# Context attention in blocks: where queries, keys, values and outputs of the next units stand among the score groups, with the seam and the first weights reordered

## The chip, the cores and the metric

The kernel runs on one core of a Trainium2 chip. A core has five engines that work side by side, each through its own list of instructions in order: TensorE (PE; its weight loads are listed apart as PEld), VectorE (DVE), ScalarE (ACT), GpSimd (POOL) and SyncE (SP, which here issues nearly all DMAs). They wait for one another through semaphores. The metric is the time of one execution in microseconds of the device; smaller is better.

## The reference

One transformer block on x, of 2 batches of 1024 rows of 256 float32 numbers, with 16 heads of 64 in both attentions. The second attention takes its keys and values from a context of 154 rows of 192 per batch.

```python
h = _layernorm(x, ln1_g, ln1_b)
x = _attention(h, h, sa_wq, sa_wk, sa_wv, sa_wo, sa_bo) + x
h = _layernorm(x, ln2_g, ln2_b)
x = _attention(h, cond_emb, ca_wq, ca_wk, ca_wv, ca_wo, ca_bo) + x
h = _layernorm(x, ln3_g, ln3_b)
p = h @ ff_w1 + ff_b1
a, gate = (p[..., :D_FF], p[..., D_FF:])
h = a * jax.nn.gelu(gate, approximate=False) @ ff_w2 + ff_b2
return h + x
```

In `_attention`, softmax(q k^T / 8) weighs v, head by head, and the heads together are multiplied by `wo`.

## The kernel before

All is float32, and the order of every engine's instructions is the order in which the program emits them. The 16 heads go in 8 pairs, so with 2 batches there are 16 *units* (batch, pair) in each attention. The kernel has four parts.

The **prologue** normalizes batch 0 and projects the first queries and keys piece by piece (`part`, `turn`, from L976 on), while weights arrive.

**Self-attention** is a loop over 128 passes p, 8 to a unit (L1026). A pass computes two score tiles (`self_first`), their maxima (DVE) and exponentials (ACT); `exchange` swaps row statistics by four small DMAs on SP; `join` and `scale_groups` put the two halves of a softmax row together (POOL, ACT, DVE); `turn_groups` transposes the probabilities on DVE; `self_values` weighs the values (tile po). Projections for the next unit, output projections and normalization run in between, handed out by `run_work`.

**Context attention** is a loop over 48 slots c, three to a unit (L1050). Each slot has one score group (`cross_first`: tile sc, maxima into neg, exponentials into p; the scaling of p by its reciprocal sums is emitted one slot later, through `lates`). A unit's groups have 3, 3 and 2 row tiles of 128, so 12, 12 and 8 matmul instructions. Two slots later DVE transposes p (`cross_drain`, `cross_turn`) into a ring of three units. Part of the transposed data is moved to other rows by eight DMAs (`cross_regroup`) into a buffer pairs, which is a part of the tile wf and exists once. `cross_values` then weighs the values in two parts of 24 instructions (tile poc). `cross_pieces` builds the next unit's queries (pq, from ca_wq), keys (pk, from ca_wk) and, for every second unit, the values of two units (pv, from ca_wv).

The **feed-forward part** has 64 slots k, each with one gate (pa) and, later, one step of the sum (pf).

What stands beside the score groups comes from four lists: `work` (projections), `side` (steps of a layer norm, some with PE transposes ph), `outs` (output projections py, 8 instructions per row tile) and `later` (DMAs and small additions, two per slot). `run_work(n, n_side, bank, n_sum)` takes up to n PSUM banks' worth of work, then side steps, then outs; `costing` says how many banks a piece takes. Two sets of two PSUM banks are used for this: `mm_tile` and `sum_tile`; score tiles have two more of two banks each. Results leave a bank through `stores` and `adds`, which `flush` emits at fixed places of a slot. In a unit of context attention the order on PE is: first group, pq; second group, poc part 0, pk, py; third group, poc part 1, pv or nothing, py.

An instruction on PE names its operand, its output and the share of the 128 by 128 array it uses: 64*128 for sc and pq (two run side by side in the two halves of the rows), 64*64 for poc and po (four side by side), 96*128 or 128*128 for pk, pv, py, ph and pa, and 96*32 for the second half of pv, whose stationary operand is the last 32 rows of the context. Each float32 product appears as two instructions.

Of the kernel before, what the change touches and what calls it, by code (L numbers as in the profile page):

```python
# [13 lines left out]
P = 128  # L14
# [4 lines left out]
def tile_transformer_block(ctx: ExitStack, tc: tile.TileContext, a: dict, out: bass.AP):  # L19
# [182 lines left out]
    spare = {"bank": mm_tile, "out": mm_tile, "keys": mm_tile}  # L202
# [436 lines left out]
    def self_beside(ui):  # L639

        parts = 2 if 0 < ui < HP else 1
        nxt = self_pieces(*units[ui + 1], parts) if ui + 1 < NU else cross_pieces(*units[0], KB)
# [31 lines left out]
    def self_drain(p):  # L674

        if joins:
            drain.append(scale_groups(*joins.pop(0)))
        if SA < p <= SA + LAG:
            turn_groups(p - LAG - 1)

# [5 lines left out]
    def cross_pieces(b, pr, m=P):  # L686

        t = {}

        def q():  # L690
            t["q"] = p2.tile([P, S], F32, tag="QT", name=f"q_ca{b}_{pr}")
            t["k"] = p2.tile([P, S], F32, tag="KT", name=f"k_ca{b}_{pr}")
            qk["ca", b, pr] = (t["q"], t["k"])
            pq = two_banks(f"pq_ca{b}_{pr}")
            project_both(pq, wsl["ca", pr, "q"], hT["ca", b], m)
            return lambda: take_both(t["q"], pq, scale)

        def keys():
            pk = spare["keys"](f"pk_ca{b}_{pr}")
            for c in range(2):  # L700
                nc.tensor.matmul(
                    pk[:, :T], lhsT=wsl["ca", pr, "k"][:, c, :],
                    rhs=ctxT[:, c, b * TP:b * TP + T], start=(c == 0), stop=(c == 1),
                )
            return lambda: nc.scalar.copy(t["k"][:, :T], pk[:, :T])

        def values():

            v = vs["ca", b, pr // 2] = pt_.tile([P, NM + 2, VC], F32, tag="V", name=f"v_ca{b}_{pr}")
            nc.vector.memset(v[:, NM:, :], 0.0)
            pv = mm_tile(f"pv_ca{b}_{pr}")
            for n, rows_ in ((0, P), (1, KB)):
                for c in range(2):
                    nc.tensor.matmul(
                        pv[:rows_, n * VC:(n + 1) * VC],
                        lhsT=ctxT[:, c, b * TP + n * P:b * TP + n * P + rows_],
                        rhs=wsl["ca", pr, "v"][:, c, :], start=(c == 0), stop=(c == 1),  # L720
                    )

            def store():
                for n in range(NM):
                    own = slice(n * QG, (n + 1) * QG)
                    nc.scalar.copy(v[own, n, :], pv[own, :VC])
                nc.scalar.copy(v[:KB, NM, :], pv[:KB, VC:])
                later.insert(0, lambda: [
                    nc.sync.dma_start(
                        out=v[(1 - n) * QG:(2 - n) * QG, n, :], in_=v[n * QG:(n + 1) * QG, n, :])  # L730
                    for n in range(NM)
                ])
                later.insert(1, lambda: [
                    nc.sync.dma_start(out=v[a4 * KB:(a4 + 1) * KB, NM + a4 % 2, :], in_=v[:KB, NM, :])
                    for a4 in range(1, P // KB)
                ])

            return store

        pieces = [costing(2, q), costing(1, keys)]  # L740
        return pieces + ([costing(1, values)] if pr % 2 == 0 else [])

# [411 lines left out]
```

## Time and profile before

| what | value |
|---|---|
| median of 3 runs | 1149.56 us (1149.43 to 1151.13) |
| profiled execution | 1148.76 us, span 1147.0 us |
| PE busy | 1120.3 us, 98% of the span |
| PE, 200 to 700 us (self-attention) | 500.0 of 500 us |
| PE, 700 to 742 us (seam of the two attentions) | 37.3 of 42 us |
| PE, 780 to 815 us | 33.7 of 35 us |
| PE, 815 to 921 us (inner units of context attention) | 106.0 of 106 us |
| ACT, 815 to 921 us | 59.0 us |
| DVE, 815 to 921 us | 68.1 us |
| DMA share, 780 to 815 us | 0.71 |

The span is the time from the first to the last instruction; the execution's own time has 1.8 us around it. A busy PE need not start its instructions as closely as it can: matmuls overlap, so the distance between starts tells more than the busy time. The timeline gives starts, merged over instructions of one line; the view of waits gives idle time of an engine and what ended it.

### The profile page before, as it was taken

The page shows a single profiled execution, that of the slowest core. Times are in us where ns is not written, and L with a number is a line of the kernel's source. Part 1 is how long each engine was busy: PE and PEld are TensorE (multiplying, and loading weights), DVE is VectorE, ACT ScalarE, POOL GpSimd, SP SyncE. Part 2 cuts the span into 40 slices and gives each one's busy share as a digit, 9 for nine tenths or more (in the row PEclk, how much of TensorE's full clock was granted, in tenths as well). Part 3 has the DMA queues.
Part 4 walks back from the last instruction along what each step waited for, and adds up shares of the span by engine and source line. Part 5 has one row for each costly group of instructions (what it writes and reads, how often), then busy time and mean ns, then how long its engine had stood idle before and what let it go on. Part 6 is the DMA issues. An engine that isn't in the chain of part 4 may idle for free.

```text
span 1147.0 us, 36735 instructions
## 1 busy us (share of the span) xinstructions
PE 1120.3 (98%) x14372; PEld 682.2 (59%) x14372; DVE 833.0 (73%) x1183; ACT 648.6 (57%) x2082; POOL 674.0 (59%) x1568
## 2 busy tenths in 40 slices
PE   8899999999999999999999999999999999999998
PEld 6444444545545545545545554566666667888887
DVE  4888899898898999999899989647666664222222
ACT  4666667666765665676666665637655571041111
POOL 2777777778777777777777777738644453020000
PEclk9999999999999999999999999999999999999999
DMA  2222112101111111111111110267554442000000
GB/s 80 68 71 66 35 32 46 41 13 40 33 29 40 31 31 44 31 31 40 31 31 40 25 28 12 52 141 208 144 120 117 116 88 56 10 10 10 19 10 19
DMA packets 104910, 59.94 MB, mean 52 GB/s; under 512 B 32090, under 2 KB 95522, under 8 KB 104738
## 3 DMA queue, kind: packets, MB, share of 16 engines
q1 hardware_dynamic: 103506, 56.93, 20.8%
q8 instruction: 114, 1.87, 0.7%
q10 hardware_dynamic: 1232, 0.66, 0.2%
q14 instruction: 58, 0.48, 0.1%
HBM read 27.91 MB, written 2.10 MB: 26 GB/s over the span
## 4 chain that ended last, share of the span: by engine, by line
PE 80%; ACT 6%; DMA 3%; DVE 3%; POOL 3%; SPq 2%; issue 2%; DVEq 0%; ACTq 0%; POOLq 0%
PE po L512 15%; PE s L465 15%; PE pa L920 10%; PE py_sa L443 5%; PE py_ca L443 5%; PE pf L943 5%; PE pq_ca L348 5%; ACT p L476 4%; PE pv_sa L379 4%; PE poc L833 4%; PE pk_sa L348 3%; PE pq_sa L348 3%; PE sc L754 3%; DMA st<-st 2%; SPq L486 2%; DVE st L626 2%
## 5 line engine op out<-in xcount | busy, mean ns | idle before, releaser
L476 ACT ACTIVATE p<-s,st 128x512 f32<-128x512 f32 x512 | 345.2, 686 | 203.2 <-DVE st L626 191.5
L577 POOL TENSOR_SCALAR p<-p,rd,ee 128x512 f32<-128x512 f32 x512 | 386.4, 771 | 44.8 <-DVE rd L573 43.9
L626 DVE TENSOR_REDUCE st<-s 128x2 f32<-128x1024 f32 x256 | 301.3, 1218 | 32.9 <-PE s L465 20.1
L591 DVE STREAM_TRANSPOSE pT<-p 128x1024 f32<-128x1024 f32 x256 | 302.1, 1218 | 0.0
L465 PE MATMUL s<-k_sa,q_sa 64*32 64x512 f32 x4096 | 252.1, 594 | 13.5 <-ACT p L476 12.8
L512 PE MATMUL po<-pT,v_sa 64*64 64x256 f32 x4096 | 235.8, 379 | 0.0
L512 PEld LDWEIGHTS po<-pT,v_sa 64*64 64x64 f32 x4096 | 150.4, 133 | 109.1 <-issue 32.8
L781 POOL TENSOR_SCALAR p<-p,rden 128x154 f32<-128x154 f32 x256 | 97.0, 401 | 98.5 <-DVE rden L778 98.0
L465 PEld LDWEIGHTS s<-k_sa,q_sa 64*32 64x32 f32 x4096 | 65.3, 106 | 137.4 <-issue 69.3
L770 ACT ACTIVATE p<-sc,neg 128x154 f32<-128x154 f32 x256 | 96.1, 396 | 79.8 <-DVE rden L778 78.1
L929 DVE SCALAR_TENSOR_TENSOR u<-pa,cols,gate 128x256 f32<-128x256 f32 x64 | 31.0, 484 | 124.4 <-ACT gate L926 124.4
L920 PE MATMUL pa<-hT_ln,wf 128*128 128x256 f32 x512 | 121.0, 379 | 0.0
L926 ACT ACTIVATE gate<-pa,cols 128x256 f32<-128x256 f32 x64 | 30.3, 474 | 151.5 <-PE pa L920 151.5
L920 PEld LDWEIGHTS pa<-hT_ln,wf 128*128 128x128 f32 x512 | 96.8, 190 | 13.7 <-DVE u L929 0.4
L476 ACT ACTIVATION_READ_ACCUMULATOR p<-s,st 128x1 f32 x512 | 103.6, 202 | 0.0
L759 DVE TENSOR_REDUCE neg<-sc 128x6 f32<-128x924 f32 (+1 forms) x48 | 48.4, 1010 | 43.1 <-PE sc L754 43.1
L379 PEld LDWEIGHTS pv_sa<-sa_wv,hT_ln 64*128 64x128 f32 x1024 | 59.3, 188 | 18.7 <-DMA st<-st 9.2
L500 POOL TENSOR_TENSOR zz<-ee,st 128x8 f32<-128x8 f32 x128 | 25.9, 203 | 67.5 <-ACT ee L498 67.5
L943 PE MATMUL pf<-wf,u 128*128 128x256 f32 x256 | 65.0, 379 | 0.2 <-DVE u L929 0.2
L379 PE MATMUL pv_sa<-sa_wv,hT_ln 64*128 64x128 f32 x1024 | 63.3, 276 | 1.7 <-DMA sa_wv<-in_L_xattn_sa_wv_dram 1.4
L443 PE MATMUL py_ca<-ca_wo,o_ca 128*128 128x256 f32 x256 | 60.8, 384 | 0.3 <-ACT hT_ln L281 0.3
L348 PE MATMUL pq_ca<-hT_ln,ca_wq 64*128 64x512 f32 (+1 forms) x304 | 60.5, 591 | 0.2 <-ACT hT_ln L281 0.2
(87 smaller groups left out, 1243.6 us busy)
## 6 DMA issues: line engine op xcount, KB each, us to landing
wf<-pT_ca SPq DMA_DIRECT2D x128, 128.0 KB, 2.4
st<-st SPq DMA_DIRECT2D x512, 1.0 KB, 1.8
v_sa<-v_sa SPq DMA_DIRECT2D x32, 256.0 KB, 3.5
sa_wq<-in_L_xattn_sa_wq_dram SPq DMA_DIRECT2D x32, 128.0 KB, 2.9
sa_wk<-in_L_xattn_sa_wk_dram SPq DMA_DIRECT2D x32, 128.0 KB, 2.8
sa_wv<-in_L_xattn_sa_wv_dram SPq DMA_DIRECT2D x32, 128.0 KB, 3.0
ca_wq<-in_L_xattn_ca_wq_dram SPq DMA_DIRECT2D x32, 128.0 KB, 3.1
wf<-in_L_xattn_ff_w_dram SPq DMA_DIRECT2D x12, 256.0 KB, 3.7
```

The costliest lines, as they stand in the source:

```text
L348: nc.tensor.matmul(pq[r][f:f + m, at:at + n], lhsT=wt[own, c, f:f + m], rhs=h[own, c, t0:t0 + n], start=(c == 0), stop=(c == NH - 1), tile ...
L379: nc.tensor.matmul(pv[r][:, i * P:(i + 1) * P], lhsT=h[own, c, i * P:(i + 1) * P], rhs=wt[own, c, :], start=(c == 0), stop=(c == NH - 1), ...
L443: nc.tensor.matmul(py[:, :D], lhsT=o[:, i, t * P:(t + 1) * P], rhs=wo[kind][:, half * HP + i, :], start=(i == 0), stop=(i == HP - 1),)
L465: nc.tensor.matmul(sc[a4 * KB:(a4 + 1) * KB, j, :], lhsT=q[r, c:c + KB], rhs=k[r, h * HB:(h + 1) * HB], start=True, stop=True, tile_positi ...
L476: nc.scalar.activation(pr[:, j, :], sc[:, j, :], AF.Exp, bias=st[:, 0, 0, i, j:j + 1], accum_out=st[:, 0, 1, i, j:j + 1],)
L512: nc.tensor.matmul(po[a2][j * DH:(j + 1) * DH, :QH // 2], lhsT=v[r, t, e, j * DH:(j + 1) * DH], rhs=pT[r, j * NK + n, :], start=(t == 0 an ...
L577: nc.gpsimd.tensor_scalar(pr[:, j, :], pr[:, j, :], rd[:, c:c + 1], ee[:, 0, c:c + 1], op0=ALU.mult, op1=ALU.mult,)
L591: nc.vector.transpose(halves[h][:, :, c:c + KB], groups.pop(0).rearrange("p j (n k) -> p (j n) k", k=KB))
L626: nc.vector.tensor_reduce(st[:, 0, 0, i, :], sc[i], AX.X, ALU.max, negate=True)
L781: nc.gpsimd.tensor_scalar(pr_[:, j, i, :T], pr_[:, j, i, :T], rden[:, j, i:i + 1], 1.0, op0=ALU.mult, op1=ALU.mult,)
L920: nc.tensor.matmul(pa[:, half, :TF * P], lhsT=w1[:, c, half * DF + f * P:half * DF + (f + 1) * P], rhs=h[:, c, t0 * P:(t0 + TF) * P], star ...
L943: nc.tensor.matmul(sums[blk][i][:, :D], lhsT=sums[blk, "u"][:, f, i * P:(i + 1) * P], rhs=w2[:, f, :], start=(f == 0), stop=(f == NF - 1),)
```

## The change

In context attention the pieces of the next unit leave `work` and stand at fixed places. The queries are computed behind the first score group of a unit. The keys come right behind the second group, and after them a norm step, the values (`context_values`, in every second unit, now for this unit and the next), two output projections, and both parts of `cross_values`; the second part takes its banks from the other set. The third group has only a norm step behind it, and output projections where more than two are waiting. The second half of pv takes the last 128 context rows instead of the last 32, and its last 32 output rows (rows 96 to 127) are kept. All eight DMAs of `cross_regroup` are issued in the third slot of the next unit. The loads of key and value weights move to the third slot. Two layer norms are queued earlier, by one unit each.

At the seam, unit 1's keys come before the first score group; the queries of units 1 and 2 behind the second and third group; the last two parts of self-attention's values behind the fourth and fifth; and the last transposes of self-attention on other places. At the start, unit 1's value weights of self-attention are loaded at the end of pass 2 and not in pass 3, one x tile goes one pass later, and in the prologue `part("k", 1)` stands before `turn[3]`.

```diff
-            halves[h, "po"] = [sum_tile(f"po_{h}_{a2}") for a2 in range(2)]
+            bank = sum_tile if h < 2 * NU - 1 else mm_tile
+            halves[h, "po"] = [bank(f"po_{h}_{a2}") for a2 in range(2)]
...
+    def cross_queries(b, pr, m=P, bank=mm_tile):
+        q = qk["ca", b, pr, "q"] = p2.tile([P, S], F32, tag="QT", name=f"q_ca{b}_{pr}")
+        pq = [bank(f"pq_ca{b}_{pr}_{r}") for r in range(2)]
+        project_both(pq, wsl["ca", pr, "q"], hT["ca", b], m)
+        return lambda: take_both(q, pq, scale)
+
+    def cross_keys(b, pr, bank=mm_tile):
+        k = qk["ca", b, pr, "k"] = p2.tile([P, S], F32, tag="KT", name=f"k_ca{b}_{pr}")
+        pk = bank(f"pk_ca{b}_{pr}")
+        for c in range(2):
+            nc.tensor.matmul(
+                pk[:, :T], lhsT=wsl["ca", pr, "k"][:, c, :],
+                rhs=ctxT[:, c, b * TP:b * TP + T], start=(c == 0), stop=(c == 1),
+            )
+        return lambda: nc.scalar.copy(k[:, :T], pk[:, :T])
+
+    def context_values(b, pr):
...
+        for n, k0 in enumerate((0, TP - P)):
+            for c in range(2):
+                nc.tensor.matmul(
+                    pv[:, n * VC:(n + 1) * VC], lhsT=ctxT[:, c, b * TP + k0:b * TP + k0 + P],
...
+        last = P // KB - 1
...
+            nc.scalar.copy(v[last * KB:, NM + last % 2, :], pv[last * KB:, VC:])
...
     def cross_regroup(c):
 
+        ui, n = divmod(c - len(CG) - 2, len(CG))
+        if n != 0 or not 0 <= ui < NU:
+            return
         for a2 in range(2):
-            ui, n = divmod(c - len(CG) - 2 - a2, len(CG))
-            if n != 0 or not 0 <= ui < NU:
-                continue
...
-        po = {a4: sum_tile(f"poc_{ui}_{a4}") for a4 in quarters}
+        po = {a4: (mm_tile if a2 else sum_tile)(f"poc_{ui}_{a4}") for a4 in quarters}
...
     def cross_beside(ui):
 
-        if ui + 1 < NU:
-            for what in "kv" if ui else "":
-                load_weights("ca", units[ui + 1][1], what)
-            pieces = cross_pieces(*units[ui + 1])
-            work.extend(pieces[:2])
-            held.extend(pieces[2:])
-        if ui == 3:
+        if ui == 2:
             norm_beside("ca", B - 1)
         if ui > HP + 1:
             ob, oh = divmod((ui - HP - 2) // HP, 2)
             t0 = ((ui - HP - 2) % HP) * 2
             out_pieces("ca", ob, oh, (t0, t0 + 1))
-        if ui == NPAIR + HP + 1:
+        if ui == NU - 4:
             norm_beside("ff", 0)
...
     def cross_weigh(c):
 
-        for part in range(2):
-            ui, n = divmod(c - len(CG) - 4 - part, len(CG))
-            if n == 0 and 0 <= ui < NU:
+        ui, n = divmod(c - 2 * len(CG) - 1, len(CG))
+        if n == 0 and 0 <= ui < NU:
+            for part in range(2):
                 run(lambda: cross_values(ui, part))
+            flush(stores)
...
         part("q", 1)
         emit(normalize[3])
         copies()
+        part("k", 1)
         copies = turn[3]()
-        part("k", 1)
...
-        later.append(tiles[0])
-        later.append(lambda: load_weights("sa", units[1][1], "v"))
-        later.extend(tiles[1:] + chunks)
+        later.extend([lambda: None] + tiles + chunks)
...
                 run_work(2 if p < SA - SH else 1, h % 2 or h == 0, sum_tile)
+                if p == LAG:
+                    load_weights("sa", units[1][1], "v")
...
-            if c % len(CG) == 0:
-                cross_beside(c // len(CG))
-            elif c % len(CG) == 1 and 1 <= c // len(CG) < NU - 2:
-                load_weights("ca", units[c // len(CG) + 2][1], "q")
-            if c % len(CG) == len(CG) - 1:
-                work.extend(held)
-                held.clear()
+            ui, n = divmod(c, len(CG))
+            nxt = units[ui + 1] if ui + 1 < NU else None
+            if n == 0:
+                cross_beside(ui)
+            elif n == 1 and 1 <= ui < NU - 2:
+                load_weights("ca", units[ui + 2][1], "q")
+            elif n == 2:
+                for i, what in ((2, "k"), (1, "v")):
+                    if 1 < ui + i < NU:
+                        load_weights("ca", units[ui + i][1], what)
+            if c == 0:
+                run(lambda: cross_keys(*nxt))
             flush(adds)
             then = cross_first(c)
             flush(stores)
+            if c == 1:
+                turn_groups(SA - 2)
+            if n == 1 and ui > 1 and nxt:
+                run(lambda: cross_keys(*nxt, sum_tile))
+                flush(stores)
             flush(drain)
             flush(lates)
             lates.append(then())
-            if c <= SH:
-                self_drain(SA + c)
+            if c == 0:
+                drain.append(scale_groups(*joins.pop(0)))
+            if c == 2:
+                turn_groups(SA - 1)
+            cross_drain(c)
+            if c == 1:
+                run(lambda: cross_queries(*nxt))
+            elif c == 2:
+                run(lambda: cross_queries(*units[2], bank=sum_tile))
+            elif c == 3:
+                run(lambda: self_values(2 * NU - 1, 0))
+            elif c == 4:
+                run(lambda: self_values(2 * NU - 1, 1))
+                run(lambda: cross_keys(*nxt, sum_tile))
+            elif n == 0 and ui:
+                if nxt:
+                    run(lambda: cross_queries(*nxt))
+                run_work(0, 1)
+            elif n == 1:
+
+                run_work(0, 1, sum_tile)
+                if ui % 2 == 0:
+                    run(lambda: context_values(*units[ui]))
+                run_work(0, 0, n_sum=1)
+                run_work(1, 0)
+                flush(adds)
+                flush(stores)
+                cross_weigh(c)
+            elif n == 2:
+                run_work(0, 1, sum_tile)
+                if len(outs) > 2:
+                    run_work(2, 0)
             cross_regroup(c)
-            cross_drain(c)
-            cross_weigh(c)
-            flush(stores)
-            if c == 1:
-
-                spare["keys"] = sum_tile
-                run_work(3, 0)
-                spare["keys"] = mm_tile
-            elif c > 1:
-                run_work(2, 1, n_sum=2 * (SH < c < 2 * NPAIR and c % len(CG) == 0))
-            if SH - LAG < c <= SH:
-                run(lambda: self_values(2 * NU - 1, c - SH + LAG - 1))
...
-            if k == 3 * len(CG):
+            if k == 3 * len(CG) - 1:
                 norm_beside("ff", B - 1)
-            cross_regroup(c)
             cross_drain(c)
             cross_weigh(c)
-            flush(stores)
+            cross_regroup(c)
             if k == 0:
                 out_pieces("ca", B - 1, 0, range(NT - 2 * TF, NT))
-            if k == len(CG) + 2:
+            if k == len(CG) + 1:
                 out_pieces("ca", B - 1, 1, range(NT))
-            if k > len(CG) + 2:
+            if k > len(CG) + 1:
                 for _ in range(min(2, len(gated) - 1)):
                     run(sum_slot)
                 flush(stores)
```

More of the change, by code (lines that the diff above doesn't have):

```diff
@@ L200, in tile_transformer_block @@
     hT, vs, qk, oT = {}, {}, {}, {}
-    spare = {"bank": mm_tile, "out": mm_tile, "keys": mm_tile}
+    spare = {"bank": mm_tile, "out": mm_tile}
     added = set()
@@ L641, in self_beside @@
         parts = 2 if 0 < ui < HP else 1
-        nxt = self_pieces(*units[ui + 1], parts) if ui + 1 < NU else cross_pieces(*units[0], KB)
+        nxt = self_pieces(*units[ui + 1], parts) if ui + 1 < NU else cross_pieces(*units[0])
         if ui + 1 < NU:
@@ L672, in load_ahead @@
             load_weights("ca", units[1][1] if p == SA - 2 else units[2][1], "kq"[p - SA + 2])
[L674 to L679, printed above, removed]
     CG = [(t, min(TG, NT - t)) for t in range(0, NT, TG)]
@@ L684, in tile_transformer_block @@
     crossed, pTc = {}, {}
[L686 to L699, printed above, removed]
+    def cross_queries(b, pr, m=P, bank=mm_tile):
[3 more added lines that the diff above has]
+        return lambda: take_both(q, pq, scale)
@@ new lines, in cross_keys @@
+    def cross_keys(b, pr, bank=mm_tile):
[8 more added lines that the diff above has]
+    def context_values(b, pr):
+        v = vs["ca", b, pr // 2] = pt_.tile([P, NM + 2, VC], F32, tag="V", name=f"v_ca{b}_{pr}")
+        nc.vector.memset(v[:, NM:, :], 0.0)
+        pv = mm_tile(f"pv_ca{b}_{pr}")
+        for n, k0 in enumerate((0, TP - P)):
@@ L700, in keys @@
             for c in range(2):
                 nc.tensor.matmul(
-                    pk[:, :T], lhsT=wsl["ca", pr, "k"][:, c, :],
-                    rhs=ctxT[:, c, b * TP:b * TP + T], start=(c == 0), stop=(c == 1),
-                )
[L705 to L738, printed above, removed]
@@ L740, in cross_pieces, with store @@
-        pieces = [costing(2, q), costing(1, keys)]
-        return pieces + ([costing(1, values)] if pr % 2 == 0 else [])
+                    pv[:, n * VC:(n + 1) * VC], lhsT=ctxT[:, c, b * TP + k0:b * TP + k0 + P],
+                    rhs=wsl["ca", pr, "v"][:, c, :], start=(c == 0), stop=(c == 1),
+                )
+        last = P // KB - 1
+        def store():
+            for n in range(NM):
+                own = slice(n * QG, (n + 1) * QG)
+                nc.scalar.copy(v[own, n, :], pv[own, :VC])
+            nc.scalar.copy(v[last * KB:, NM + last % 2, :], pv[last * KB:, VC:])
+            later.insert(0, lambda: [
+                nc.sync.dma_start(
+                    out=v[(1 - n) * QG:(2 - n) * QG, n, :], in_=v[n * QG:(n + 1) * QG, n, :])
+                for n in range(NM)
+            ])
+            later.insert(1, lambda: [
+                nc.sync.dma_start(
+                    out=v[a4 * KB:(a4 + 1) * KB, NM + a4 % 2, :],
+                    in_=v[last * KB:, NM + last % 2, :])
+                for a4 in range(last)
+            ])
@@ L743, in cross_first, with cross_pieces @@
+        return store
+    def cross_pieces(b, pr):
+        return [costing(2, lambda: cross_queries(b, pr, KB)), costing(1, lambda: cross_keys(b, pr)),
+                costing(1, lambda: context_values(b, pr))]
     def cross_first(c):
@@ L747, in cross_first @@
         t0, nt = CG[n]
-        q, k = qk["ca", b, pr]
-        k = k[:, :T]
+        q, k = qk["ca", b, pr, "q"], qk["ca", b, pr, "k"][:, :T]
         sc = ps_s.tile([P, 2, HB], F32, tag="s", name=f"sc_{c}")
```

## The prediction

> **What bounds the kernel now.** I read the page first: one core, TensorE clock at full speed in every slice, so time is instructions and waits.
>
> ```profile
> span 1147.0 us, 36735 instructions
> PE 1120.3 (98%) x14372; PEld 682.2 (59%) x14372; DVE 833.0 (73%) x1183; ACT 648.6 (57%) x2082; POOL 674.0 (59%) x1568
> ```
>
> PE is the bound; a change pays only if it takes waits out of PE or makes its instructions start closer together. The view of waits comes next, for PE alone:
>
> ```profile
> PE s L465 <- ACT p L476: 12.8, 22, 1.6
> PE sc L754 <- ACT k_ca L705: 2.3, 1, 2.3
> PE ph_ln L266 <- POOL xn_ln L253: 2.2, 3, 1.1
> PE pv_sa L379 <- DMA sa_wv<-in_L_xattn_sa_wv_dram: 1.4, 2, 1.0
> ```
>
> Two belong to what is changed: 2.3 us at the seam, for context keys, and 1.4 us at the start, for value weights. The rest must come from closer starts, so I read PE's timeline over one inner context unit (score groups at 849.55, 853.87, 858.65). Columns: start, busy time, line, output<-inputs, rows*columns of the array, operand.
>
> ```profile
> 849.55 1.06 PE L754 MATMUL sc<-k_ca,q_ca 64*128 64x154 f32 x12
> 850.43 3.60 PE L348 MATMUL pq_ca<-hT_ln,ca_wq 64*128 64x512 f32 x16
> 853.87 0.95 PE L754 MATMUL sc<-k_ca,q_ca 64*128 64x154 f32 x12
> 854.75 1.09 PE L833 MATMUL poc<-wf,v_ca 64*64 64x256 f32 x16
> 855.66 0.61 PE L833 MATMUL poc<-pT_ca,v_ca 64*64 64x256 f32 x8
> 856.21 0.79 PE L701 MATMUL pk_ca<-ctxT,ca_wk 96*128 96x154 f32 x4
> 856.83 1.89 PE L443 MATMUL py_ca<-ca_wo,o_ca 128*128 128x256 f32 x8
> 858.65 0.79 PE L754 MATMUL sc<-k_ca,q_ca 64*128 64x154 f32 x8
> 859.38 1.09 PE L833 MATMUL poc<-wf,v_ca 64*64 64x256 f32 x16
> 860.29 0.61 PE L833 MATMUL poc<-pT_ca,v_ca 64*64 64x256 f32 x8
> 860.84 2.11 PE L717 MATMUL pv_ca<-ca_wv,ctxT 96*128 96x256 f32 x8
> 862.88 1.99 PE L443 MATMUL py_ca<-ca_wo,o_ca 128*128 128x256 f32 x8
> 864.80 1.06 PE L754 MATMUL sc<-k_ca,q_ca 64*128 64x154 f32 x12
> ```
>
> Read differences of starts. Eight py take 1.82 us behind pk (856.83 to 858.65) but 1.92 behind pv (862.88 to 864.80). In the FF stage, among full-array neighbours only, sixteen take 3.45 (985.68 to 989.13), so eight 1.73. The excess is paid where the array's division changes.
>
> **Term 1, changes of division.** Call F full (96 or 128 rows, 128 columns: pk, pv, py, ph, pa), R 64*128 (sc, pq), Q 64*64 (poc, po). Leaving F costs 1.82 - 1.73 = 0.09; entering F 1.92 - 1.82 = 0.10. Twelve sc take 0.88 behind py and before pq; 24 take 1.67 (719.50 to 721.17), so twelve alone are 0.79, entering R costs 0.10 (rounded up), and leaving it as much (0.88 at 853.87). Sixty-four po take 3.61 (732.93 to 736.54) and 24 poc 1.46, so 0.215 per four; 24 without edges would be 1.30, edges 0.16: by the single starts 0.05 in, 0.11 out. Hence F to R or R to F 0.20, R to Q or F to Q 0.15, Q to F or Q to R 0.21. The second half of pv is 96*32: pv and py from 860.84 to 864.80 take 3.96, against 1.73 twice plus 0.19 of edges, 3.65: 0.31 for the narrow half, gone in the new code, where both halves have 128 columns.
>
> An inner unit now changes six times: F-R, R-Q, Q-F, F-R, R-Q, Q-F = 1.12, plus 0.31 where it has pv. The new order is sc, pq, sc, pk, (pv), py, py, poc twice, sc: R-F, F-Q, Q-R = 0.56, and none at the border of units, where sc meets sc. Where a py pair or a transpose stands behind the third group, two more, 0.40. Following the lists of work through all units from 742 to 948: now 31 F-R, 28 R-Q, 28 Q-F, 4 R-F, one Q-R and seven narrow halves, 19.4 us; new 6 F-R, 21 R-F, 14 F-Q, 14 Q-R, 10.4. That is -9.0. In the FF stage two visits of poc instead of four save 2 x 0.36 = -0.7.
>
> The Trainium skill, "TensorEngine Tiling (Array Packing)", Key Properties, says that changing the tiling mode drains the TensorE; "TensorE: Matmul & The Clock Gate", Part 2, puts a drain at about 128 cycles of 2.4 GHz. By an estimate from those pages the 54 changes saved are 54 x 53 ns = 2.9 us; the rows make it 9.6, and the sum keeps the rows. Against the change, Part 3 of the second page has weight loads overlap with running matmuls only in other row groups, and Part 2 makes them proportional to columns: by that estimate the wider pv half would add (128 - 32)/1.2 ns x 4 x 7 = 2.2 us. The trace disagrees: full py and pa start 0.216 us apart, each with its 0.19 us load hidden.
>
> **Term 2, waits from 742 to 948.** PE's stretch is 206.1 us. Its work without edges, counts by the starts above (228 sc pairs x 0.131, 13 pq x 3.43, 13 pk x 0.53, 7 pv and 28 py x 1.73, 28 poc x 1.30, 8 ph x 0.43), is 181.5; with 19.4 of edges, 5.2 of waits are left, nearly all beside the two layer norms (780 to 815, 921 to 948). New ones: sc of group three and of the next unit's first group are adjacent, so ScalarE has the exponentials of both in a row. VectorE puts a maximum (0.80), a reciprocal and a transpose pair (1.2) before the second maximum (1.12): those exponentials start 3.6 us into the unit instead of 2.3 (864.80 to 867.14), take 2.2, and the query copies (0.56 each) follow. pv wants the bank of the first copy, free at 6.4; PE arrives at 0.79 + 3.43 + 0.88 + 0.63 = 5.7. So 0.65 in four inner units with pv, 2.6 in all; without pv the sum bank of py covers it. The norm steps come in as many slots, and one starts a unit earlier: I take 3.4 for theirs. In all 6.0, +0.8; bounds 2 and 12.
>
> What hides the rest: the moved poc copies (0.72 a part, VectorE) end before pq needs those banks, 0.8 us later; were they late, PE would wait one copy, 0.36, a unit. The memset, the value copies and their five DMAs (the last chunk now from rows 96 to 127, same sizes) have a unit and a half before poc reads them. On SP, all eight regroup issues now stand in one row behind the end of poc, past the loads of k and v; four took 2.62 at 856.93, so eight 5.2, and landing 2.4 (page) makes 7.6. The next poc comes 10.0 (no pv) later: cover 2.4 us. Behind the regroup on SP waits the query load, wanted 10 us on. POOL keeps its order and all instructions.
>
> **Term 3, the seam: 0.** Keys of unit 1 now come before the first score group, so PE waits for their weights:
>
> ```profile
> 718.72 1.48 SPq L120 DMA_DIRECT2D ca_wk<-in_L_xattn_ca_wk_dram  x1
> ...
> 728.51 1.06 PE L754 MATMUL sc<-k_ca,q_ca 64*128 64x154 f32 x12 [2.29 <-ACT k_ca L705]
> ```
>
> PE is there at 719.50. The 512-byte packets of that load run from 721.0 to 721.8, so pk starts near 722.1: a wait of 2.6 in place of 2.29, with everything behind it queued on PE. Bounds: 720.7 (2.0 after issue, the 64 KB copies of v_ca) and 724.71, where pk ran without waiting. Then pk, two sc, pq, sc, pq, sc end at 732.6; po needs the last self-attention transposes. Their chain (exponential 727.4, reciprocal 728.5, four POOL scalings 3.02, transposes) ends at 732.9: 0.3 more. po, sc, po, pk bring the third group of unit 1 to 741.85, now 741.86. The swapped banks (queries of unit 2 in sum banks, the last po in the others) are free 2 us ahead. Bounds -1.5 and +2.
>
> **Term 4, the start: -1.6.** The load of unit 1's value weights moves from behind the fourth exchange on SP (issued 44.10) to behind the third (37.74). PE then does not wait 0.40 + 0.97; but the fourth exchange is issued 0.5 later, and score pass 6 needs the exponentials behind it: -1.0 (0 to -1.4). The one x tile loaded later is wanted four passes on. In the prologue part k 1 moves ahead of the fourth transposes, into waits of 0.1 and 0.19 and past one pair of edges: s starts at 17.85 instead of 18.44, -0.6 (0 to -0.7). From 200 to 700 PE has no gap, so a lead stays.
>
> **Sum.** -9.0 - 0.7 + 0.8 + 0 - 1.6 = -10.5. The profiled execution took 1148.76 (span 1147.0 and 1.8 around it), giving 1138.3; the shown median, 1149.56, lies 0.8 above: 1139.1.
>
> **Rivals.** (a) Slower: the eight regroup issues come late for poc. With the slowest four (3.63 at 742.02) twice and the longest landing in the trace, 5.7 (ca_wk), it is 13.0 against 10.0 or 11.7: waits of 3.0 and 1.3 by turns, 14 units, 30 us: 1169. It decides from 0.75 us a unit, a landing 11.6 us after poc. For: one queue, DMA up to 74% busy. Against: that load falls on units 2 to 5, where most have 4 us more. Chance 0.09. (b) ScalarE becomes the bound of the unit: 0.8 us of waiting in all 13 units with pq, +10.4 less the 2.6 counted: 1147, or no change with term 4 lost, 1149. Against: ScalarE is busy 59.0 of 106 us there. Chance 0.10. (c) Half the good: norm waits double (+3.4), keys' weights land late (+2), start unmoved (+1.6): 1146. Chance 0.18. (d) The change of division costs nothing when queues refill: then only terms 3 and 4, 1148; the repeated start differences speak against. 0.03. Forecast: 0.60.
>
> **How the numbers follow.** 0.2% (2.3 us) is what can be told from no change. The forecast's own bounds: waits of 2 and term 4 at -2.1, seam -1.5, give 1133; waits of 12, no gain at the start and seam +2 give 1148.7. That holds (b) and (c) too; I take 1133.5 to 1148.5 and leave out (a) and the ends. Faster: forecast, (c), most of (b): 0.85; same: (d) and the rest of (b), 0.05; slower: (a) and the tail, 0.10.
>
> **What would show it.** Right: poc x48 in one run, no 96*32 loads, sc followed by sc; an inner unit pair of about 27.7 us instead of 28.5; PE idle before pk near 720; no pv_sa wait on DMA. Wrong: PE waits on DMA before poc, on the ACT query copy before pv beyond 1 us, or pv longer than 1.83.

## The result, and the profile after

The changed kernel is slower. Its median is 1153.77 us (1152.21 to 1154.88), beside 1149.49 us (1147.95 to 1151.13) for the kernel before: a ratio of 1.0039, 95% interval 1.0026 to 1.0052. A second comparison, at the end of the experiments, gave 1.0041 (1.0026 to 1.0055). The loss of 0.4% is small, but clear of the noise. Predicted were 1139.1 us, a ratio of 0.991, and a range from 1133.5 to 1148.5 us. All ratios here are of fast executions; one slow execution of 3067 us, of the kernel with the norm step behind the values, is left out of its ratio.

The page of the changed kernel: the span is 4.9 us longer, and PE is busy 3.9 us *less*. So PE waits more; it does not work more.

```profile
span 1151.9 us, 36754 instructions
PE 1116.4 (97%) x14372; PEld 687.6 (60%) x14372; DVE 836.3 (73%) x1183; ACT 646.6 (56%) x2082; POOL 675.9 (59%) x1568
```

The view of PE's waits after the change (engine, line, releaser: total us, times, longest):

```profile
PE poc L825 <- ACT hT_ln L281: 5.8, 3, 3.0
PE pv_ca L706 <- ACT q_ca L363: 2.9, 6, 1.2
PE pk_ca L690 <- DMA ca_wk<-in_L_xattn_ca_wk_dram: 2.3, 1, 2.3
PE pv_sa L379 <- ACT k_sa L371: 1.3, 1, 1.3
```

The first of these is new and large: the weighing of the values waits three times for a *layer norm's* copies. It lies in units 4, 5 and 15. Here are units 4 and 5 (timeline: start, busy, engine, line, and in brackets the wait ahead and what ended it):

```profile
784.61 0.60 PE L266 MATMUL ph_ln<-ident,xn_ln 128*128 128x128 f32 x4
...
788.23 1.60 ACT L281 ACTIVATE hT_ln<-ph_ln,cols 128x128 f32<-128x128 f32 x4
789.88 1.22 PE L825 MATMUL poc<-wf,v_ca 64*64 64x256 f32 x10 [1.73 <-ACT hT_ln L281]
...
801.45 0.60 PE L266 MATMUL ph_ln<-ident,xn_ln 128*128 128x128 f32 x4
...
804.40 1.66 ACT L281 ACTIVATE hT_ln<-ph_ln,cols 128x128 f32<-128x128 f32 x4
806.11 0.86 PE L825 MATMUL poc<-wf,v_ca 64*64 64x256 f32 x10 [2.99 <-ACT hT_ln L281]
```

The transposes ph end at 785.2, but ScalarE takes them out of their bank only from 788.23 on: the copies stand on its list behind the query copies, the key copy and six exponentials. That bank is one of the two summing banks, and the first part of poc needs both.

In the kernel before, the transposes of such a step take a bank of the other set and stand *behind* the first part of poc, and neither part waits:

```profile
786.52 1.09 PE L833 MATMUL poc<-wf,v_ca 64*64 64x256 f32 x16
...
788.60 0.60 PE L266 MATMUL ph_ln<-ident,xn_ln 128*128 128x128 f32 x4
...
789.86 1.09 PE L833 MATMUL poc<-wf,v_ca 64*64 64x256 f32 x16
```

A second loss follows. Stretches of time in the same place (columns: busy time of PE, PEld, DVE, ACT, POOL, then the granted clock, DMA share, GB/s):

```profile
780.00:790.00 10.00, 7.90 (x52) 4.82 (x52) 6.71 (x16) 9.51 (x41) 9.60 (x26) 1.00 0.89 236
790.00:800.00 10.00, 10.00 (x86) 5.98 (x88) 6.04 (x13) 4.70 (x22) 5.20 (x13) 0.83 0.58 136
800.00:810.00 10.00, 6.60 (x70) 4.12 (x66) 3.26 (x7) 6.05 (x27) 4.17 (x13) 0.87 0.84 195
```

The clock was granted in full everywhere in the profile before. After the change the trace's clock record drops to one half for 3.413 us from 790.3 and again from 807.3, right behind the two waits, and once in the start, from 97.4.

The inner unit, on the other hand, is what the prediction said (same view as its unit of before):

```profile
838.12 1.58 PE L746 MATMUL sc<-k_ca,q_ca 64*128 64x154 f32 x20
839.53 3.60 PE L348 MATMUL pq_ca<-hT_ln,ca_wq 64*128 64x512 f32 x16
842.97 0.95 PE L746 MATMUL sc<-k_ca,q_ca 64*128 64x154 f32 x12
843.85 0.79 PE L690 MATMUL pk_ca<-ctxT,ca_wk 96*128 96x154 f32 x4
844.97 1.99 PE L706 MATMUL pv_ca<-ca_wv,ctxT 96*128 96x256 f32 x8 [0.33 <-ACT q_ca L363]
846.80 3.62 PE L443 MATMUL py_ca<-ca_wo,o_ca 128*128 128x256 f32 x16
850.35 1.09 PE L825 MATMUL poc<-wf,v_ca 64*64 64x256 f32 x16
```

Such double score groups (the third group of a unit and the first of the next, 20 instructions) start at 825.47, 838.12 and 853.10: a pair of units takes 27.63 us, against 28.47 before and 27.7 predicted.

Every run below is placed by one table of *offsets*: the start of the same PE instruction in the run's profiled execution, minus its start in that of the kernel before (us from each span's start). Negative is earlier. "Pass 127" is the last pass of self-attention, c a slot of context attention (12 and 18 enclose units 4 and 5; 42 begins unit 14), "ff 0" the first gate. The last column is where the clock record drops to one half within the program, each time for 3.41 us (6.83 where marked *); a drop at the very end of the program is left out.

| kernel | pass 127 | c=5 | c=12 | c=18 | c=42 | ff 0 | end | half clock from |
|---|---|---|---|---|---|---|---|---|
| changed | +1.15 | +0.86 | -2.03 | +4.56 | +0.74 | +4.38 | +4.93 | 97, 790, 807 |
| changed, again | +1.43 | +2.32 | -0.56 | +6.87 | +3.00 | +6.61 | +7.17 | 35, 185, 724, 792, 806* |
| norm step behind | +0.76 | +0.26 | -0.13 | -2.11 | -1.70 | -0.51 | +0.04 | 97, 704 |
| norm copies first | -1.24 | -0.08 | -2.97 | -2.32 | -5.97 | -4.05 | -3.50 | 722 |
| waits filled | +0.83 | +0.38 | -2.51 | +0.69 | -3.17 | +0.44 | +1.00 | none |
| ff outputs moved | +0.10 | -0.56 | -3.44 | +3.91 | +0.04 | +3.65 | +3.04 | 35, 789, 803* |
| single column | -0.46 | -1.49 | -3.80 | +4.58 | +3.03 | +7.15 | +8.30 | 35, 789*, 806 |
| before, new start | +0.14 | +0.23 | +0.23 | +0.22 | +0.22 | +0.20 | +0.20 | 35 |
| before, new prologue | +2.40 | +3.99 | +3.99 | +3.98 | +3.98 | +3.96 | +3.96 | 35, 185, 731 |
| before, wide pv | +1.38 | +1.30 | +0.87 | +0.60 | -0.35 | -0.05 | -0.05 | none |
| three moves | +1.87 | +2.92 | +0.04 | +0.69 | -5.53 | -2.95 | -3.57 | 725 |
| and keys earlier | +2.90 | +0.69 | -2.19 | -1.54 | -7.13 | -2.87 | -3.48 | 97, 186, 923 |
| last version | +2.99 | +0.51 | -2.37 | -1.43 | -7.63 | -5.69 | -6.30 | 35, 185 |

For the changed kernel: +1.15 in the start, -0.29 in the seam, -2.89 to unit 4, +6.59 in units 4 and 5, -3.82 in units 6 to 13, +3.64 in units 14 and 15, +0.55 behind. The two large losses are where a layer norm runs.

### The profile page after: what moved, and what is told of

Same layout as the page of the kernel before. It is cut to its first block, busy times and chain, and to the rows that moved or that the text cites. A ratio compares the mean times of both kernels' runs of the same rounds, so it can differ in the third digit from the quotient of the medians.

```text
span 1151.9 us, 36754 instructions
## 1 busy us (share of the span) xinstructions
PE 1116.4 (97%) x14372; PEld 687.6 (60%) x14372; DVE 836.3 (73%) x1183; ACT 646.6 (56%) x2082; POOL 675.9 (59%) x1568
## 3 DMA queue, kind: packets, MB, share of 16 engines
q8 instruction: 114, 1.87, 0.7%
## 4 chain that ended last, share of the span: by engine, by line
PE 80%; ACT 7%; DVE 4%; DMA 3%; issue 2%; POOL 2%; SPq 2%; DVEq 0%; ACTq 0%; POOLq 0%
PE po L512 17%; PE s L465 17%; PE pa L907 10%; PE py_sa L443 5%; PE pf L930 5%; PE py_ca L443 4%; PE pk_sa L348 4%; PE pq_sa L348 4%; PE poc L825 4%; PE pv_sa L379 4%; ACT p L476 3%; PE pq_ca L348 3%; ACT p L762 2%; PE sc L746 2%; DMA st<-st 2%
## 5 line engine op out<-in xcount | busy, mean ns | idle before, releaser
L773 POOL TENSOR_SCALAR p<-p,rden 128x154 f32<-128x154 f32 x256 | 97.4, 404 | 101.2 <-DVE rden L770 100.7
L762 ACT ACTIVATION_READ_ACCUMULATOR p<-sc,neg 128x1 f32 x256 | 59.8, 233 | 0.0
L443 PE MATMUL py_ca<-ca_wo,o_ca 128*128 128x256 f32 x256 | 58.3, 381 | 1.3 <-DVE o_ca L838 1.0
```

Source lines behind the costliest of these rows:

```text
L443: nc.tensor.matmul(py[:, :D], lhsT=o[:, i, t * P:(t + 1) * P], rhs=wo[kind][:, half * HP + i, :], start=(i == 0), stop=(i == HP - 1),)
L762: nc.scalar.activation(pr_[:, j, i, :T], sc[:, j, i * T:(i + 1) * T], AF.Exp, bias=neg[:, j, i:i + 1], accum_out=den[:, j, i:i + 1],)
```

## The experiments

The **theory**, formed from the profile above: a summing bank is held by norm transposes whose copies queue behind exponentials ("held bank"), and the waits cost clock besides. The **rival**: ScalarE has too much work there, so any reordering only moves the wait (the prediction's rival (b), at the norm units).

### The norm step behind the values

```diff
-                run_work(0, 1, sum_tile)
                 if ui % 2 == 0:
                     run(lambda: context_values(*units[ui]))
...
                 cross_weigh(c)
+                run_work(0, 1, sum_tile)
```

> The changed kernel, but the norm step of a unit's second slot (transposes into a summing bank) stands behind the two joined visits of values instead of ahead of them. Theory 'held bank': in units 4, 5 and 14 the first visit waits for a bank that the transposes hold until ScalarE has copied them out, and ScalarE does that behind six exponentials. The waits 1.73, 0.42, 2.99 and 1.07 us ahead of the visits go (6.2 us), and with them the two half-speed stretches of 3.41 us at 788 and 805 us that follow them (1.7 us each): 1153.8 - 6.2 - 3.4 = 1144.2 us, between 1142 and 1147. Rival 'ScalarE too slow': from 742 to 948 us the work on ScalarE is too much for the time, so the wait only moves to the next reader of ScalarE; 1152 to 1154 us.

Measured: 1150.88 us, ratio 1.0002 (0.9992 to 1.0012). About 4 us of the 9.6 came. The waits of poc for the norm are gone, and with them the half clock at 790 and 807: units 4 and 5 went from +6.59 to -1.98. But a unit earlier (c=5 to c=12) 2.5 us were lost again, and between c=18 and c=42 another 4.2, of which 2.4 are waits ahead of c=42. None of these waits had been there; the longest of each place:

```profile
780.09 0.66 PE L266 MATMUL ph_ln<-ident,xn_ln 128*128 128x128 f32 x4 [1.85 <-POOL xn_ln L253]
...
919.07 0.33 PE L266 MATMUL ph_ln<-ident,xn_ln 128*128 128x128 f32 x1 [1.35 <-ACT xn_ln L256]
```

A step transposes what the step before it normalized. Moved back, it stands only one score group behind that step, and the normalization (on POOL for this layer norm, on ScalarE for the next) isn't done. The place was wrong, not the theory: ScalarE has the same work here and lost nothing by it in units 4 and 5.

### The norm step in its place, its copies ahead of the exponentials

```diff
             if n == 1 and ui > 1 and nxt:
                 run(lambda: cross_keys(*nxt, sum_tile))
                 flush(stores)
+            if n == 1 and c > SH:
+                run_work(0, 1, sum_tile)
+                flush(stores)
             flush(drain)
             flush(lates)
             lates.append(then())
```

> The changed kernel with the norm step of the second slot still ahead of the values and in the same summing bank, but issued before the group's exponentials, so that ScalarE copies the transposes out first and then takes the exponentials. It parts two causes inside 'held bank'. If it is the queue on ScalarE (copies behind six exponentials, about 3.5 us) that keeps the bank, the waits ahead of the visits go as in the run with the step moved behind: 1144 to 1147 us, less good by up to 2 us because the exponentials start 1.6 us later. If the bank is too short whatever the order, the first visit still waits over 1 us in units 4 and 5 and the time is 1151 to 1154 us. 'ScalarE too slow' gives 1152 to 1154 us here too.

Measured: 1145.18 us, ratio 0.9952 (0.9938 to 0.9966), the ScalarE work being the same. This parts the causes: it is the *order* on ScalarE. (PE's list is the same. The step's few instructions on VectorE and POOL come earlier too; that it is the copies which freed poc is read from the rows.) The copies now come from 785.07 on, 0.8 us behind the transposes, and what is left of the waits in units 4 and 5 is this, but for 0.41 us on the key copy:

```profile
784.63 1.99 PE L706 MATMUL pv_ca<-ca_wv,ctxT 96*128 96x256 f32 x8 [0.36 <-ACT q_ca L363]
785.07 1.57 ACT L281 ACTIVATE hT_ln<-ph_ln,cols 128x128 f32<-128x128 f32 x4
...
789.88 0.87 PE L825 MATMUL poc<-wf,v_ca 64*64 64x256 f32 x10 [1.38 <-ACT v_ca L716]
...
800.87 0.86 PE L825 MATMUL poc<-wf,v_ca 64*64 64x256 f32 x10 [0.75 <-ACT hT_ln L281]
```

The next in line in unit 4 is the second part of poc, which waits for the values' copies, now behind the exponentials themselves. Units 4 and 5 give +0.65 in place of +6.59, units 14 and 15 +1.92 in place of +3.64; 2.4 us of this profile's lead are from the start (pass 127), of which more below.

### The waits filled with idle work

```diff
+                if ui in (4, 5):
+                    fill = mm_tile(f"fill_{c}")
+                    for _ in range(12 if ui == 4 else 22):
+                        nc.tensor.transpose(fill[:, :P], ident, ident)
                 cross_weigh(c)
```

> The changed kernel with 12 and 22 transposes of a constant, whose result nobody reads, put ahead of the joined visits of units 4 and 5, in a bank of the other kind, so that TensorE works through the two waits of 1.73 and 2.99 us. Nothing is made earlier. Theory 'idle costs clock': the two stretches at half clock (3.41 us each, at 788 and 805 us) come from these waits; filled, the clock stays whole there and the time falls by 2 x 1.7 = 3.4 us to 1150.4, with up to 1 us taken back where the filling lasts longer than the wait (1150 to 1152). Rival 'the clock falls for another reason': the half-speed stretches stay, and the time is 1153.8 to 1155.

Measured: 1150.40 us, ratio 0.9995 (0.9987 to 1.0004). Windows as above, and the waits that are left:

```profile
790.00:800.00 10.00, 10.00 (x103) 6.72 (x95) 7.23 (x16) 6.44 (x29) 6.46 (x17) 1.00 0.53 119
800.00:810.00 10.00, 8.95 (x99) 6.31 (x99) 4.87 (x11) 5.42 (x26) 3.87 (x12) 1.00 0.94 216
...
789.38 0.86 PE L825 MATMUL poc<-wf,v_ca 64*64 64x256 f32 x10 [0.41 <-ACT hT_ln L281]
...
803.89 0.86 PE L825 MATMUL poc<-wf,v_ca 64*64 64x256 f32 x10 [1.05 <-ACT hT_ln L281]
```

The granted clock is 1.00 in both, and units 4 and 5 cost +3.20 instead of +6.59: 3.4 us less, as expected, though not one useful instruction was made earlier. These two waits cost twice: their length, and 1.7 us of slow clock each.

### A price for a change of the array's division

```diff
+        if a2:
+            k = P if ui % 2 == 0 else QG
+            nc.tensor.matmul(
+                po[a2][:k, NT * KB:NT * KB + 1], lhsT=ident[:k, :k], rhs=ident[:k, :1],
+                start=True, stop=True, **({} if k == P else {"tile_position": (0, 0)}),
+            )
```

> The changed kernel with one matmul of a single column between the two joined visits of every unit: over the whole array (128 by 128) in even units, over a quarter of it (64 by 64, as the visits themselves) in odd units. It is a price for a change of the array's division by itself. Theory 'edges cost': the quarter-sized one costs its own issue, some 0.05 us; the whole one costs that and two changes, 0.35 to 0.45 us, so the two visits together last about 0.35 us longer in even units than in odd ones, and the program about 8 x 0.4 + 8 x 0.05 = 3.6 us longer (waits aside). Rival 'edges cost nothing': even and odd units alike within 0.1 us.

Measured once, 1157.05 us, which tells nothing finer than the profile does. The same single column between the two parts, over the whole array and over a quarter:

```profile
850.93 1.09 PE L831 MATMUL poc<-wf,v_ca 64*64 64x256 f32 x16
...
852.39 0.38 PE L822 MATMUL poc<-ident 128*128 128x1 f32 x2
...
854.16 1.58 PE L746 MATMUL sc<-k_ca,q_ca 64*128 64x154 f32 x20
...
864.06 1.09 PE L831 MATMUL poc<-wf,v_ca 64*64 64x256 f32 x16
...
865.41 0.16 PE L822 MATMUL poc<-ident 64*64 64x1 f32 x1
...
866.91 1.58 PE L746 MATMUL sc<-k_ca,q_ca 64*128 64x154 f32 x20
```

From poc to sc it is 3.23 us in the even unit and 2.85 in the odd one; the plain visit takes 2.75 (850.35 to 853.10 above). So a quarter-sized matmul costs 0.10 and a whole one 0.48. The difference, 0.38, is at most the price of the two changes, where the prediction's prices give 0.21 + 0.15 = 0.36. Part of it may be the whole matmul's own: its two instructions start 0.13 us apart, each with its weight load, and those of the quarter 0.03. Without that it is 0.28. Rival (d), no price at all, is out either way.

### The context values alone

```diff
-            for n, rows_ in ((0, P), (1, KB)):
+            for n, k0 in enumerate((0, TP - P)):
```

(the kernel before, with the copies and DMAs of the last rows as in the change)

> The kernel before with the context values' last 32 rows computed by a matmul over the whole array (128 rows that overlap the first 128) instead of one over 32 columns of it; nothing else. By rows of the profile before, the narrow matmul had a change of division behind it, so the 8 visits save about 0.3 us each, of which the prediction took 2.2 us in all: 1147.3. By the rule that four times the weights' columns take four times as long to load, it would lose 2.2 us: 1151.7. If the visits' time is hidden or the same either way: 1149.3 to 1149.7.

Measured: 1148.31 us, ratio 0.9986 (0.9977 to 0.9995), 1.6 us faster. In its trace pv and py of an inner unit take 1.83 + 1.82 = 3.65 us, where they took 3.96 before and 3.65 was predicted; the offset falls by 0.31 a visit in the inner units. By the estimate that spoke against the wider pv it would have been slower.

### The start

Two kernels: the kernel before with the whole new start (the x tile one pass later too; the weights at the end of pass 2, the third), and with its prologue alone.

```diff
+        part("k", 1)
         copies = turn[3]()
-        part("k", 1)
...
+                if p == LAG:
+                    load_weights("sa", units[1][1], "v")
```

> The kernel before with the changed start alone (the second key part ahead of the fourth turn in the prologue; the first value weights loaded at the fifth pass instead of with the first loads). In the changed kernel's profile the start is 0.9 us early in the prologue and 1.15 us late from pass 35 on, with a half-speed stretch at 95 to 98.6 us. Theory 'the start costs': 1149.5 + 1.15 = 1150.6 us, between 1150.2 and 1151.5, with that half-speed stretch there again. Rival 'the prediction's': the weights' wait of 1.0 us and 0.6 us of the prologue are gained, 1147.9. Rival 'chance of that execution': no difference, 1149.3 to 1149.7.

> The kernel before with the second key part ahead of the fourth turn alone, the loads as before. Parts the two halves of the start. If the late pass 9 to 15 comes from the moved weights, this keeps the gain of the prologue, 0.6 to 0.9 us: 1148.6 to 1148.9. If the earlier prologue itself shifts the exchange of bytes between partitions into the loads and so costs the half-speed stretch, it is 1150 to 1151.5 as the whole start is.

Measured: 1150.13 us, ratio 1.0009 (0.9997 to 1.0020), and 1150.47 us, ratio 1.0001 (0.9993 to 1.0010). Neither is told from no change; the gain that the prediction took, to 1147.9, is excluded for the whole start, a cost of 1.1 us is not. The first score does start earlier in every profile with the new prologue (by 0.4 to 0.9 us), but the lead does not last. Eleven profiles with the whole new start, the same instructions up to pass 123, stand from -1.24 to +2.99 us at pass 127. One with the old start, that of the wide pv, stands at +1.38. So the +1.15 of the changed kernel, and the 2.4 us by which the run with the copies first led there, are within what one execution and the next differ by, and not to be put down to the change. The half-speed column shows much of the chance: the stretches at 35, 97 and 185 us come and go.

### The feed-forward part

```diff
-            run_work(2, 1)
+            weighed = k in (1, len(CG) + 1)
+            run_work(0 if weighed else 2, 1, n_sum=2 * weighed)
```

> The changed kernel with the two output pieces that stand behind each joined visit in the feed-forward part taken into summing banks, whose copies are a visit earlier, instead of into the banks that the second visit has just filled. Theory: the two waits of 0.51 us on VectorE's copies go and the gain predicted for that part comes out, 1153.8 - 1.0 = 1152.8 us. Rival: the pieces then wait for VectorE all the same (it adds the earlier pieces first) or the following sums wait for the banks, and nothing changes: 1153.5 to 1154.2.

Measured: 1151.80 us, ratio 1.0015 (1.0006 to 1.0023), against 1.0039 and 1.0041 unmended. In the changed kernel the outputs behind the joined parts waited for the second part's banks:

```profile
962.80 3.72 PE L443 MATMUL py_ca<-ca_wo,o_ca 128*128 128x256 f32 x16 [0.51 <-DVE o_ca L838]
```

This wait and its like at 974.97 are gone: from ff 0 to the end the offset moves by -0.61 in place of +0.55, so 1.2 us, and the -0.7 that was predicted for this part comes out. The ratios differ by some 2.8 us; where the rest comes from, the profiles do not tell, and the start's differences are of that size.

### A version from these parts, in three steps

First: norm copies first, outputs in summing banks, and the context values behind the first output piece (only this last move is shown).

```diff
+                run_work(0, 0, n_sum=1)
                 if ui % 2 == 0:
                     run(lambda: context_values(*units[ui]))
-                run_work(0, 0, n_sum=1)
```

> The changed kernel with three moves together: norm step of the second slot ahead of the exponentials; context values behind the unit's first output piece, so that they don't wait for the copies of the queries; the two output pieces behind the joined visits of the feed-forward part in summing banks. From the parts: the run with the norm step ahead gave a ratio of 0.9952 to the kernel before; the waits of the values on the query copies (0.33 us four times and 1.21 us once) make 2.5 us at most, the two waits in the feed-forward part 1.0 to 1.2 us. If they add up: 0.9952 - 3.6/1150 = 0.992, some 1140.5 us; if the values' wait only moves on to the second visit, which needs their bank, 0.9942, some 1143 us.

Measured: 1144.70 us, ratio 0.9953 (0.9938 to 0.9968), less than expected. The waits of pv in the inner units are gone (c=18 to c=42: -6.22, where -3.65 came with the copies alone), but in unit 14 the first output waits 1.87 us for the bank of the keys instead of pv's 1.21. In the profiled execution the start took the rest of it: +1.87 at pass 127, where the run with the copies alone had -1.24. The half-speed stretch near 725 stands in both.

Second: the keys' weights one pass earlier.

```diff
-        if p >= SA - 2:
-            load_weights("ca", units[1][1] if p == SA - 2 else units[2][1], "kq"[p - SA + 2])
+        if p in (SA - 3, SA - 1):
+            load_weights("ca", units[1][1] if p == SA - 3 else units[2][1], "kq"[p == SA - 1])
```

> As the run before it, and the keys' weights of the second unit loaded one pass earlier, ahead of the last two exchanges of the first attention on SP's queue. It tells what sets the seam. If the 2.29 us that the keys wait for their weights is the transfer's place in the queue, they go, and the time is another 2 us lower, 1138 to 1141 us; if what stands behind them (values of the last half, whose transposed weights come through the same queue, or ScalarE's exponentials) is late next, the wait is given back within the seam and the time is that of the run before it, within 0.5 us.

Measured: 1143.30 us, ratio 0.9945 (0.9932 to 0.9958), above the 1138 to 1141 that were expected and, by the intervals, not told from the step before. In the profile the wait at the seam is gone. The load is issued at 714.80 (first row; second row, the changed kernel, 719.87), and PE passes from po to pk without a wait:

```profile
714.80 1.23 SPq L120 DMA_DIRECT2D ca_wk<-in_L_xattn_ca_wk_dram  x1
...
719.87 1.46 SPq L120 DMA_DIRECT2D ca_wk<-in_L_xattn_ca_wk_dram  x1
...
718.79 3.68 PE L512 MATMUL po<-pT,v_sa 64*64 64x256 f32 x64
722.40 0.79 PE L690 MATMUL pk_ca<-ctxT,ca_wk 96*128 96x154 f32 x4
```

From pass 127 to c=5 the offset moves by -2.21, in the changed kernel by -0.29; nothing is late in its place. The transfer's place in SP's queue set the seam.

Third: in unit 4, which has no outputs, pv behind poc; in unit 14 pv ahead of the outputs again.

> The version with the keys' weights loaded earlier, and two places mended that its profile shows: in unit 4, which has no output pieces, the context values stand behind the joined visits, so that the second visit does not wait 1.39 us for ScalarE to copy them out of its bank, nor they 0.36 us for the queries' copies; in unit 14, where the first output piece waited 1.87 us for a bank that the keys hold, the values stand ahead of it again and wait 1.21. If these waits go and none comes in their place: 2.4 us less than the version before it, a ratio of 0.9945 - 0.0021 = 0.9924, some 1140.9 us. If the values of unit 4 now wait for VectorE's copies of the second visit (0.5 us, as the output pieces did in the feed-forward part) and two changes of the array's division are added (0.4 us), 1 us of it is left and the ratio is about 0.9935.

Measured: 1142.37 us, ratio 0.9934 (0.9917 to 0.9951), near the second of the expected values, though not for its reasons. By the table 2.3 us came back in units 14 and 15 (1.7 of it the half-speed stretch at 923 behind the wait of 1.87). From c=12 to c=42 only 0.3 us were gained: in unit 4 PE now comes to the first part of poc earlier, since pv no longer stands ahead of it, and waits there, 1.04 us for the key copy and 0.76 for the norm's copies. This is the lowest ratio of all, though its interval overlaps with the two before it; it is 7 us under the kernel before and 12 under the change as it was made:

```profile
span 1140.7 us, 36752 instructions
PE 1114.8 (98%) x14372; PEld 688.6 (60%) x14372; DVE 835.5 (73%) x1183; ACT 646.9 (57%) x2082; POOL 676.1 (59%) x1568
```

The changed kernel itself was run once more beside these:

> The changed kernel as it is, beside the runs of this call. In the profiles so far the end of the first attention stands between 1.2 us early and 1.2 us late against the kernel before though all but one of these kernels have the same instructions up to there. If that is chance of the execution (the place of a half-speed stretch in the first 100 us), this one falls anywhere in that span, and the ratio is 1.0039 within 0.0015. If it is the changed start, it is 1.0 to 1.3 us late again.

Measured: 1154.93 us, ratio 1.0041 (1.0026 to 1.0055), with +1.43 at pass 127. That alone would suit either reading; the kernel before with the new start (+0.14) and the spread of the eleven speak for chance, and leave room for a cost of about 1 us. The loss in units 4 and 5 is there again, +7.43, with half clock at 792 and 806.

## Why the prediction was wrong

**Term 1, right.** The changes of the array's division cost what their rows said: 27.63 us an inner pair for 27.7, 0.28 to 0.38 for two changes for 0.36, 3.65 for pv and py for 3.65. PE's list of instructions in the changed kernel has the predicted counts (6 F-R, 21 R-F, 14 F-Q, 14 Q-R). So the -9.0 of context attention is in the changed kernel, and the last version keeps it.

**Term 2, the step that failed.** "The norm steps come in as many slots, and one starts a unit earlier: I take 3.4 for theirs." The changed kernel takes 209.64 us from the third group of unit 1 to ff 0 (742.72 to 952.36); less the work of 181.5 and the changes' 10.4 that is 17.7 us of waits and slow clock, for 6.0 predicted and a bound of 12. (The counts and times listed for the work add up to 181.7, not 181.5; both remainders fall by 0.2.) The trace shows where it went: PE's idle time in this stretch is 10.4 us, 2.3 before, and 3.4 us are slow clock. These are 11.5 of the 12.5 us that the remainder grew by. The predicted 3.4 was a share of the old waits carried over, not a walk through the new order. In that order the transposes take a summing bank *just ahead* of poc, which needs both, and the bank comes free only behind the query copies, the key copy and six exponentials: in unit 4 its copies begin 3.0 us after the transposes end. In units 12 to 15 output pieces stand between and hide most of it; in units 4 and 5 there are none, and it is 5.1 us of waiting. Both were to be read in the code and the durations of before. To this comes what no term had, 3.4 us of half clock. The other part of term 2, pv's wait on the query copies, was right in kind and nearly in size: 0.33 us of idle and some 0.5 of start distance four times, for 0.65, and 1.2 in unit 14. The signs that the prediction set for being wrong watched that wait, not the one that decided.

**Term 1's last part, FF, mis-sized by a wait:** -0.7 of changes came, but the joined second part of poc holds the banks that the outputs want, 2 x 0.51 and a little more: +0.55. That copies of poc "end before pq needs those banks" was true only where pq stands next.

**Term 3, right.** The seam came to -0.29 for 0. A wait of 2.29 us was replaced by one of 2.29, and the last versions show that it could be removed.

**Term 4, not confirmed.** -1.6 was taken; the new start alone gives a ratio of 1.0009 (0.9997 to 1.0020), so at most a third of a microsecond of gain. The first score starts at least 0.4 us earlier and the wait of pv_sa on its weights is gone, but in six of the eleven profiles pv_sa then waits 1.0 to 1.3 us for ScalarE's key copies (the fourth line of waits above). And the wait of 1.4 us was read from one execution: the two other profiles with the old loads (wide pv, new prologue) do not have it, and are later at pass 127 all the same. "A lead stays" from 200 us on is so, but what the first 200 us make of it is chance within about 4 us.

**The rivals.** (a) is out: no wait on a DMA ahead of poc. (b) is out as put: with the same ScalarE work in another order the time is 1145.2. (c), waits doubled, had the mechanism's kind; it was the right rival at too small a size, and none of the cases took it past the kernel before. Of the chance of 0.10 for slower, 0.09 was the regroup.

**The whole.** By the offsets: -9.0 of changes and +12.5 of waits and slow clock in context attention, +1.15 in the start, -0.29 in the seam, +0.55 behind make the +4.9 us of this profile. The +1.15 is within chance; the rest is slower without it.

## What to carry to other kernels

When pieces move together, write down for each bank who fills it, who empties it, and what stands ahead of the emptying instruction on its engine; do this for the units where the usual filler between them is missing, since those decide. Where a small copy frees something PE is about to need, issue it ahead of the long run of exponentials: it is the order on ScalarE that counted here, with its busy share at 56% of the whole all along, and above 9 of 10 us in the window from 780 in both orders. And a wait of PE of 1.7 us or more can cost another 1.7 us of slow clock: of 22 such waits in these profiles (the first one, at 2 us, left out) 13 stand at a half-speed stretch, among them all four of about 3 us.

## What the hardware showed

The half-speed stretches are of one kind. In all profiles the record changes in steps of 3.413 us. If PE's idle time (by its modelled ends) is summed over the step ahead of each drop, 27 of 27 drops to half clock stand behind a step with 1.52 to 3.33 us of idle time. Over the 14 profiles, steps with 1.74 us or more were followed by a drop 18 times of 19, steps between 1.50 and 1.73 us 9 times of 26, steps with less never. So about half a step idle can be enough, and the same wait is punished or not by where the grid falls: the waits near 96 us (one of 1.5 us, and shorter ones) gave half clock in three of the profiles and not in the others. A stretch costs 1.7 us, so this is a part of what differs between profiles here. One thing stays open: the stretch at 789 of the run with the single column lasted a second step, though PE was never idle in its first. "TensorE: Matmul & The Clock Gate" of the Trainium skill, Part 1, describes a free-running window of 3413 ns; the steps in the records are of that length. Its advice to avoid idle gaps above some 3 us (section "Why this matters for your kernels") is too wide for this case: gaps of 1.7 us did it, as those of 1.72 and 1.73 us in unit 4 did in four of the profiles.
